# The causal mask of the first key block: from a TensorE product to selections and products on the exponentials

## The chip, the cores and the metric

The kernel runs on one core of a Trainium2 chip. The core has five engines, each of which works through its own queue in order: TensorE (PE; its weight loads are shown as PEld), VectorE (DVE), ScalarE (ACT), GpSimd (POOL) and SyncE (SP, which here only issues transfers). Matrix products are written to PSUM, eight banks of 128 x 512 fp32; all else lies in SBUF. GpSimd does not work on PSUM in this kernel.

The metric is the device time of one execution in microseconds. The kernel before takes 3545.71 us, the median of three runs (3545.69, 3545.71, 3548.17). One more execution was profiled.

## The reference

The input is 32 sequences of 256 tokens with 256 features. First comes a state-space block (a projection, a short convolution, a layer norm, a clipped recurrence over the 256 tokens with 16 states of 512 channels, a gate, a projection back). On its result work two transformer layers with local attention over windows of 128 and a gated feed-forward network. The attention is what the change touches:

```python
def local_attention(q, k, v):                    # 8 heads of 64; WINDOW = 128, so w = 2 windows
    bq = q.reshape(b, h, w, WINDOW, d) * QK_SCALE
    bk, bv = (look_around(bk), look_around(bv))  # the window before, and the own one
    sim = jnp.einsum('bhwid,bhwjd->bhwij', bq, bk)
    mask = (i < j) | (i > j + WINDOW) | (j == -1)
    sim = jnp.where(mask, -jnp.finfo(sim.dtype).max, sim)
    attn = jax.nn.softmax(sim, axis=-1)
    out = jnp.einsum('bhwij,bhwjd->bhwid', attn, bv)
```

With 256 tokens there are two key blocks. The keys of block 0 are seen by the queries of window 0 where the query is not earlier than the key, and by those of window 1 where the query is at most 128 later. So the 128 x 256 scores of key block 0 (keys by queries) keep an upper triangle of the left half and a lower triangle of the right half. Key block 1 is seen by window 1 alone, with one triangle.

## The kernel before

The 32 sequences go in four groups of eight (`NG`, `GB`). For one group `group_scan` (from L379) runs the state-space block: 256 steps, one after the other, each one VectorE instruction over 128 x 512 (`step`, L718) on a row that ScalarE scales (L708) and TensorE reads out (L730). In chunks of 32 steps it prepares the convolution: GpSimd starts an accumulator (`conv_in`, L480), VectorE adds three taps (`conv_taps`, L491). Then the group's eight sequences pass through two layers, so there are 4 x 2 x 8 = 64 passes of one sequence through one layer. The state-space block of group g + 1 runs beside the passes of group g. The last group's 16 passes have nothing beside them.

A pass is spread over eight stages (`ST = 8`), by `attend`, `feed` and `fetch` (L1485 to L1532), and neighbouring passes overlap: while one pass makes scores, the next sequence is projected, the output of the one before is finished, and older ones are in the feed-forward network. What matters here, by stage of pass n:

- Stages 0 to 6, for the next sequence: `project` makes q, k and v of both windows on TensorE (`ps_qkv`, L991); `rotated` (L1000) squares them on ScalarE (L1004), applies the rotary tables on VectorE (L1007, L1012, L1017) and GpSimd (L1015, and the inverse norm `rn` in L1021); `unit` (L1027, VectorE) scales. The second window's rotations are written in stage 4.
- Stage 2: `scores` of the first two head pairs of key block 0 and of all four pairs of key block 1. Stage 3: `scores` of the last two head pairs of key block 0. Scores go into two PSUM banks (one for each head of a pair), and `exponentials` (L1239, ScalarE) turns each bank into an SBUF tile `pT` of 128 x 512. There are six `pT` buffers, as many as one pass uses.
- Stage 3: `mask` of key block 1 by GpSimd's `affine_select` (L1250).
- Stage 7: `sums` (the softmax denominators, L1264) and `values` (L1282), both TensorE on `pT`.
- In the next pass: the denominators go through DRAM and come back inverted and spread (stages 0 to 3), `divide` (stage 5) multiplies the attention output `oT` by them on VectorE (L1322), `finish` (stage 6) projects it (`ps_wo`, L1047).
- Also feed-forward work: gelu products on VectorE (`ag`, L1420), the last addition `fo` of the second layer on VectorE (L1440) and, with the input, on GpSimd (L1448).

The mask of key block 0 is made in two ways. In groups 0 to 2 `open_banks` (L1200) first multiplies a bf16 unit matrix by a bf16 mask of 0 and -32768 into the bank, 128 x 512 for each of the four banks of a pass, and `products` adds the scores on top. Since half of each triangle's square is masked anyway, `products` splits the 128 keys in two halves of 64 and leaves the fully masked quarter out: four matmuls of 64 x 64 weights and 192 queries for a head pair. In the last group (`self.apart`) there is no mask product, a head pair takes two matmuls of 64 x 128 weights and 256 queries, and VectorE multiplies the exponentials by a mask of 0 and 1 (L1255), twice in each of stages 3 and 4.

The program's text gives an order, and a planner makes each engine's queue from it by the dependences and by durations that it estimates: an instruction whose inputs it expects early can be issued ahead of earlier text. `tc.keep_in_program_order` pins an instruction behind everything written before it for its engine. The masks, `divide` and `unit` are pinned so; the rotations and convolution steps are not.

## Time and profile before

| what | value |
|---|---|
| median of three runs | 3545.71 us |
| the profiled execution, its own time | 3553.66 us |
| its span in the trace | 3551.9 us |
| granted TensorE clock, mean | 0.986 |
| busy: TensorE / VectorE / ScalarE / GpSimd | 97% / 73% / 57% / 46% |
| mask products L1200: 192, mean duration | 380 ns |
| score products L1227 of 64 x 64 weights and 192 queries: 1536 records | 335 ns |
| score products L1227 of 64 x 128 weights and 256 queries: 256 records | 402 ns |
| selections L1250, 128 x 512: 128, mean | 853 ns |
| mask products of VectorE L1255, 128 x 512: 64, mean | 817 ns |

The recurrence of the first group runs alone up to about 480 us. From then to about 2790 us passes and recurrence run side by side, and from there to the end the last group's passes run alone.

How to read it: a matmul's duration contains the time to fill and drain the array, and neighbours overlap, so the cost of a row of matmuls is read from its first start to the start of what follows. fp32 matmuls appear as two records each. Waits name the instruction that came last; "idle before" of an engine that is not the bound costs nothing. In order-of-time views the columns are start and duration in us, engine, line, operation, output and inputs, shape, count, and in brackets the idle time before and what ended it.

### The profile page before, as it was taken

What the parts mean: (1) busy time and instruction counts of PE and PEld (TensorE: products, weight loads), DVE (VectorE), ACT (ScalarE), POOL (GpSimd) and SP (SyncE); (2) the same over time, 40 slices, a digit from 0 to 9 for tenths busy, and PEclk for the clock granted to TensorE, in tenths of its full rate; (3) what the DMA queues carried; (4) which work ended last, traced back from release to release, by engine and by line L of the source; (5) the groups of instructions that cost most, each with busy time, mean ns of one, the idle gap of its engine ahead of it and who ended that gap; (6) DMA issues with size and microseconds to landing.
All of it is one profiled execution on the core that took longest, in us unless ns stands there. A gap on an engine that the chain in (4) does not pass through costs nothing.

```text
span 3551.9 us, 57690 instructions
## 1 busy us (share of the span) xinstructions
PE 3441.7 (97%) x20220; PEld 2263.7 (64%) x20220; DVE 2605.5 (73%) x5049; ACT 2037.4 (57%) x3663; POOL 1620.7 (46%) x1587
## 2 busy tenths in 40 slices
PE   7999989999999999999999999999999999999999
PEld 5445335666666666666666666666666777777777
DVE  4888898877878777877787778787777545555563
ACT  3666656656666656666566656666666444444442
POOL 4433455544545445544454556454443333333441
PEclk8999999999999999999999999999999999999999
DMA  6788765534454555544454445544444212011111
GB/s 183 211 219 217 200 174 153 135 113 134 125 143 138 150 144 150 139 121 126 123 144 131 139 147 146 145 115 129 124 138 118 63 37 62 13 31 35 37 28 38
DMA packets 487199, 436.72 MB, mean 123 GB/s; under 512 B 247155, under 2 KB 326516, under 8 KB 486772
## 3 DMA queue, kind: packets, MB, share of 16 engines
q1 hardware_dynamic: 402450, 420.94, 42.0%
q10 hardware_dynamic: 84450, 12.01, 2.1%
q8 instruction: 162, 2.65, 0.3%
q14 instruction: 137, 1.12, 0.1%
HBM read 384.06 MB, written 47.19 MB: 121 GB/s over the span
## 4 chain that ended last, share of the span: by engine, by line
PE 64%; DVE 16%; DMA 7%; ACT 5%; POOL 4%; issue 3%; SPq 1%; ACTq 0%; DVEq 0%; POOLq 0%
PE ps_qkv L991 13%; PE pa L1402 13%; PE po_f L1429 6%; DVE h L718 6%; DMA xrep<-xnd 5%; PE y L730 5%; PE ps_wo L1047 5%; PE ov L1282 4%; PE ps_in L401 3%; PE ps_out L810 3%; PE sc L1227 3%; PE tr_qk L1036 2%; PE rs L1264 2%; ACT xrep L708 2%; DVE acc L491 2%
## 5 line engine op out<-in xcount | busy, mean ns | idle before, releaser
L718 DVE CUSTOM_DVE_ANT_0 h<-h,xrep,lim 128x512 f32<-128x512 f32 x1024 | 931.9, 910 | 215.1 <-ACT xrep L708 166.5
L708 ACT ACTIVATE xrep<-xrep,beta 128x512 f32<-128x512 f32 x960 | 672.5, 720 | 315.7 <-DMA xrep<-xnd 202.4
L991 PE MATMUL ps_qkv<-qkv,res 128*128 128x512 f32 x1536 | 715.2, 601 | 17.2 <-DVE ag L1420 7.2
L1402 PE MATMUL pa<-hT,w 128*128 128x256 f32 (+1 forms) x2816 | 674.5, 382 | 5.4 <-DVE zT L801 5.1
L1402 PEld LDWEIGHTS pa<-hT,w 128*128 128x128 f32 (+1 forms) x2816 | 517.6, 189 | 145.1 <-issue 38.0
L1015 POOL TENSOR_TENSOR rot<-rot,swp 128x512 f32<-128x512 f32 x256 | 349.0, 1363 | 543.7 <-DVE swp L1012 513.0
L991 PEld LDWEIGHTS ps_qkv<-qkv,res 128*128 128x128 f32 x1536 | 282.2, 191 | 299.8 <-issue 242.2
L1021 POOL TENSOR_TENSOR rn<-ss,neg_half 128x8 f32<-128x8 f32 x256 | 461.0, 1801 | 0.0
L1420 DVE SCALAR_TENSOR_TENSOR ag<-pa,b_sb,ag 128x256 f32<-128x256 f32 x320 | 151.9, 475 | 280.0 <-ACT ag L1413 279.7
L730 PE MATMUL y<-h,ly 128*32 128x512 f32 x2048 | 335.8, 606 | 9.8 <-DVE h L718 9.2
L1429 PE MATMUL po_f<-ag,w 128*128 128x256 f32 x1280 | 305.7, 386 | 1.4 <-DVE fo L1440 0.6
L1354 POOL TENSOR_TENSOR rstd<-ve,neg_half 128x2 f32<-128x2 f32 x64 | 46.1, 720 | 555.9 <-DVE ve L1352 555.9
L1429 PEld LDWEIGHTS po_f<-ag,w 128*128 128x128 f32 x1280 | 235.3, 190 | 64.8 <-DVE xc L511 11.7
L1413 ACT ACTIVATE ag<-pa,b_sb 128x256 f32<-128x256 f32 x320 | 149.9, 469 | 217.8 <-PE pa L1402 215.7
L1004 ACT ACTIVATE sq<-ps_qkv,tiny 128x512 f32<-128x512 f32 x256 | 172.4, 685 | 172.2 <-PE ps_qkv L991 143.8
L1047 PE MATMUL ps_wo<-oT,wo 128*128 128x256 f32 x1024 | 236.2, 385 | 14.2 <-DVE oT L1322 11.2
L1047 PEld LDWEIGHTS ps_wo<-oT,wo 128*128 128x128 f32 x1024 | 196.6, 193 | 45.5 <-issue 9.9
L491 DVE SCALAR_TENSOR_TENSOR acc<-xr,wc_sb,acc 128x256 f32<-128x256 f32 x384 | 188.6, 523 | 46.4 <-POOL acc L480 45.9
L1012 DVE TENSOR_TENSOR swp<-ps_qkv,rs_sb 128x256 f32<-128x256 f32 x512 | 191.8, 416 | 29.8 <-POOL rot L1015 29.6
L1007 DVE TENSOR_TENSOR rot<-ps_qkv,rc_sb 128x512 f32<-128x512 f32 x256 | 173.8, 679 | 45.8 <-ACT sq L1004 45.6
L1239 ACT ACTIVATE pT<-sc 128x512 f32<-128x512 f32 x384 | 202.1, 603 | 7.3 <-PE sc L1227 5.5
L1027 DVE SCALAR_TENSOR_TENSOR rot<-rn,rot 128x512 f32<-128x512 f32 x256 | 196.1, 804 | 5.0 <-POOL rn L1021 4.7
(161 smaller groups left out, 5306.9 us busy)
## 6 DMA issues: line engine op xcount, KB each, us to landing
xrep<-xnd SPq DMA_DIRECT2D x960, 256.0 KB
rb<-inv SPq DMA_DIRECT2D x128, 256.0 KB
xnd<-xn SPq DMA_DIRECT2D x64, 256.0 KB
qkv<-in_wqkv_dram SPq DMA_DIRECT2D x24, 512.0 KB
ahead<-xs_a SPq DMA_DIRECT2D x48, 256.0 KB
xp<-ahead SPq DMA_DIRECT2D x48, 256.0 KB
xd<-xnd SPq DMA_DIRECT2D x192, 64.0 KB
w<-in_w_dram SPq DMA_DIRECT2D x80, 128.0 KB
```

Of the source, the lines that this page charges most:

```text
L491: nc.vector.scalar_tensor_tensor(acc, xr[:, :, k : k + CH], wc_sb[:, ch, k : k + 1], acc, ALU.mult, ALU.add,)
L708: scaled = nc.scalar.activation(bx, ck[c].pop(("bx", t), bx), AF.Copy, scale=ck[c]["beta"][:, t : t + 1])
L718: nc.vector._custom_dve(TENSOR_ADD_SAT, out=h_new, in0=state["h"], in1=bx, s0=ck[c]["lim"][:, 0, t : t + 1], s1=ck[c]["lim"][:, 1, t : t + 1],
L730: nc.tensor.matmul(ck[c]["y", hb][32 * q : 32 * q + 32, :], ly[hb % 2][:, 32 * t : 32 * t + 32], ck[c].pop(("h", hb * TB + t)), start=(i = ...
L991: nc.tensor.matmul(ps, res[b][:, k, t0 : t0 + W], wt["qkv", a][:, k], start=(k == 0), stop=(k == KM - 1),)
L1015: nc.gpsimd.tensor_add(rot, rot, swp)
L1021: nc.gpsimd.tensor_tensor(rn, ss, neg_half, ALU.pow)
L1027: nc.vector.scalar_tensor_tensor(rot, bc(rn, 2, DH), 1e12, rot, ALU.min, ALU.mult)
L1047: nc.tensor.matmul(po[:, d], wt["wo", 0][:, c, d * P : (d + 1) * P], oT[:, c, :], start=(c == 0), stop=(c == NC_ - 1),)
L1239: nc.scalar.activation(p, banks[r], AF.Exp)
L1402: nc.tensor.matmul(dst[x], wt["w1", m][:, k, x], self.h[:, k], start=(k == 0), stop=(k == KM - 1),)
L1429: nc.tensor.matmul(self.po[:, d], wt["w2", 0][:, m, d * P : (d + 1) * P], self.ag[m], start=(m == 0), stop=(m == len(MCH) - 1),)
```

## The change

No group makes the mask product any more. `products` takes two matmuls of 64 x 128 weights and 256 queries for a head pair in every group. The mask of key block 0 is put on the exponentials: in groups 0 to 2 the first two head pairs (written in stage 3) by VectorE's product with the mask of 0 and 1, the last two (stage 4) by GpSimd's selection, two `affine_select` for each of two tiles, each over one half of the queries (128 x 2 x 128). In the last group both stay on VectorE. The bf16 unit matrix and the mask of -32768 go, and the mask of 0 and 1 is made directly.

```diff
-    mask_t = const.tile([P, 2 * W], BF, tag="mask_t", name="mask_t")
-    ident_b = const.tile([P, P], BF, tag="ident_b", name="ident_b")
-    nc.vector.tensor_copy(ident_b, ident)
-    nc.gpsimd.memset(mask_t, 0.0)
...
     mask_1 = const.tile([P, 2 * W], BF, tag="mask_1", name="mask_1")
-    nc.gpsimd.tensor_scalar(mask_1, mask_t, -1.0, None, ALU.is_ge)
+    nc.gpsimd.memset(mask_1, 1.0)
+    for i, sign in enumerate((1, -1)):
+        half_1 = mask_1[:, i * W : (i + 1) * W]
+        nc.gpsimd.affine_select(
+            out=half_1, in_=half_1, compare_op=ALU.is_ge, fill=0.0,
+            base=0, pattern=[[sign, W]], channel_multiplier=-sign,
+        )
...
-                self.apart = g == NG - 1
+                self.l, self.last = l, g == NG - 1
...
             def open_banks(self, kw, n):
                 nq = S - kw * W
-                banks = []
-                for r in range(2):
-                    sc = ps_w.tile([P, n, nq], FP, tag="w", name="sc")
-                    if kw == 0 and not self.apart:
-                        nc.tensor.matmul(
-                            sc, ident_b, bc(mask_t[:, 0:nq], 1, n), start=True, stop=False
-                        )
-                    banks.append(sc)
-                return banks
+                return [ps_w.tile([P, n, nq], FP, tag="w", name="sc") for _ in range(2)]
...
-                        for m in range(nm):
-
-                            k0 = m * mk
-                            q0, q1 = (k0, k0 + W + mk) if masked else (0, nq)
-                            nc.tensor.matmul(
-                                banks[r][k0 : k0 + mk, i, q0:q1],
-                                kT[rows, i0 + i, kw * W + k0 : kw * W + k0 + mk],
-                                qT[rows, i0 + i, kw * W + q0 : kw * W + q1],
-                                start=not masked,
-                                stop=not masked or i == n - 1,
-                            )
+                        nc.tensor.matmul(
+                            banks[r][:, i, :],
+                            kT[rows, i0 + i, kw * W : (kw + 1) * W],
+                            qT[rows, i0 + i, kw * W :],
+                            start=True,
+                            stop=True,
+                        )
...
-                    if kw:
-                        masked = nc.gpsimd.affine_select(
-                            out=p, in_=p, compare_op=ALU.is_ge, fill=0.0, base=0,
-                            pattern=[[0, n], [1, W]], channel_multiplier=-1,
+                    if kw == 0 and (i0 == 0 or self.last):
+                        tc.keep_in_program_order(
+                            nc.vector.tensor_mul(p, p, bc(mask_1[:, 0:nq], 1, n))
                         )
-                    else:
-                        masked = nc.vector.tensor_mul(p, p, bc(mask_1[:, 0:nq], 1, n))
-                    tc.keep_in_program_order(masked)
+                        continue
+                    for j in range(nq // W):
+                        sign, part = 1 - 2 * j, p[:, :, j * W : (j + 1) * W]
+                        tc.keep_in_program_order(
+                            nc.gpsimd.affine_select(
+                                out=part, in_=part, compare_op=ALU.is_ge, fill=0.0,
+                                base=0, pattern=[[0, n], [sign, W]],
+                                channel_multiplier=-sign,
+                            )
+                        )
...
             stage(n, 3, at.mask, 1, 0)
-            if at.apart:
-                for i, what in ((3, (0, 0)), (4, (0, 2))):
-                    stage(n, i, at.mask, *what)
+            for i, what in ((3, (0, 0)), (4, (0, 2))):
+                stage(n, i, at.mask, *what)
```

## The prediction

> **What bounds the kernel now.** I read the page first: one line of it says who is full.
>
> ```profile
> PE 3441.7 (97%) x20220; PEld 2263.7 (64%) x20220; DVE 2605.5 (73%) x5049; ACT 2037.4 (57%) x3663; POOL 1620.7 (46%) x1587
> ```
>
> A share over the whole span mixes stages, so the next view is the table of stretches (columns: us, busy of PE, PEld, DVE, ACT and POOL, granted TensorE clock, DMA share, GB/s).
>
> ```profile
> 780.00:800.00 20.00, 18.24 (x131) 13.27 (x132) 16.53 (x26) 7.60 (x14) 7.30 (x7) 0.84 0.56 143
> 980.00:1000.00 20.00, 17.19 (x66) 10.15 (x65) 12.76 (x21) 10.32 (x18) 6.92 (x5) 0.91 0.46 115
> 1800.00:2000.00 200.00, 198.06 (x1240) 131.52 (x1240) 159.61 (x316) 124.96 (x229) 105.80 (x99) 1.00 0.48 134
> ```
>
> From 1000 to 2850 us TensorE idles about 1%, VectorE 20%, GpSimd nearly half. TensorE is the bound there, and what leaves it is worth its length, as long as nothing that it waits for gets later. How near is that? Third view, the waits of TensorE:
>
> ```profile
> PE ps_wo L1047 <- DVE oT L1322: 11.2, 4, 6.1
> ```
>
> The total is small, but a wait list shows no near misses. So the fourth view is the order of time, VectorE and then TensorE, around one output projection `ps_wo` (I number the 64 passes of a sequence through a layer from 0; this is pass 29's):
>
> ```profile
> 2055.19 1.21 DVE L1322 TENSOR_TENSOR oT<-oT,rb 128x1024 f32<-128x1024 f32 x1
> 2056.33 0.68 DVE L1007 TENSOR_TENSOR rot<-ps_qkv,rc_sb 128x512 f32<-128x512 f32 x1
> ...
> 2060.38 0.80 DVE L718 CUSTOM_DVE_ANT_0 h<-h,xrep,lim 128x512 f32<-128x512 f32 x1
> ```
>
> ```profile
> 2054.74 1.99 PE L1402 MATMUL pa<-hT,w 128*128 128x256 f32 x8
> 2056.57 3.67 PE L1047 MATMUL ps_wo<-oT,wo 128*128 128x256 f32 x16
> ```
>
> The division `oT` ends at 2056.40 and `ps_wo` starts at 2056.57: no slack. Measured so for all passes, the distance is 0.05 to 0.27 us at 1, 4, 6, 8, 11, 13, 15, 17, 27, 29, 31 and 33, 1.3 to 1.5 at the other odd ones from 19 to 37, and 1.7 to 9.7 at nearly all even ones. Odd passes carry the recurrence's convolution on VectorE, and there VectorE is right behind TensorE.
>
> **The change, part by part.** *TensorE.* The trace has both forms: groups 0 to 2 open the first key block with mask products, the last group does not. In order of time:
>
> ```profile
> 2033.38 0.59 PE L1200 MATMUL sc<-mask_t,ident_b 128*128 128x512 bf16 x2
> 2033.91 1.97 PE L1227 MATMUL sc<-qT,kT 64*64 64x192 f32 x32
> 2035.81 2.42 PE L1429 MATMUL po_f<-ag,w 128*128 128x256 f32 x10
> ...
> 2038.94 0.59 PE L1200 MATMUL sc<-mask_t,ident_b 128*128 128x512 bf16 x2
> 2039.47 0.88 PE L1227 MATMUL sc<-qT,kT 64*64 64x192 f32 x16
> 2040.28 1.98 PE L991 MATMUL ps_qkv<-qkv,res 128*128 128x512 f32 x4
> ...
> 3131.91 2.02 PE L1227 MATMUL sc<-qT,kT 64*128 64x256 f32 x24
> 3133.86 2.43 PE L1429 MATMUL po_f<-ag,w 128*128 128x256 f32 x10
> ...
> 3137.09 1.13 PE L1227 MATMUL sc<-qT,kT 64*128 64x256 f32 x8
> 3138.15 1.98 PE L991 MATMUL ps_qkv<-qkv,res 128*128 128x512 f32 x4
> ```
>
> From the first scores' start to the next work's, stage 2 falls from 2.43 to 1.95 us and stage 3 from 1.34 to 1.06: 0.75 a pass by the medians over all (0.76 here), times 48 passes, **-36.0 us**. Nothing covers it: this is the bound. In the first ten passes (500 to 1000 us, TensorE busy 469 of 500) part of their 7.5 us may be lost. I count it whole.
>
> *Added work.* VectorE gets two products a pass, and GpSimd four selections over half the width (duration in ns: least, median, most):
>
> ```profile
> L1255 DVE TENSOR_TENSOR pT<-pT,mask x64: 679/683/1764, 2904.0 to 3486.6; 128x512 f32<-128x512 f32 x64
> ...
> L1250 POOL TENSOR_SCALAR_AFFINE_SELECT pT<-pT x128: 628/812/1212, 520.9 to 3480.6; 128x512 f32<-128x512 f32 x128
> ```
>
> That is 2 x 0.683 = 1.37 us on VectorE (66 us in all) and 4 x 0.43, half a selection's mean of 0.853, = 1.7 us on GpSimd (82 us in all). As load alone both fit the idle shares, and the masked tiles are wanted only in stage 7 (in one pass scores at 1538.9, sums at 1562.1 us). What counts is what they push. The products are issued just ahead of `unit` (L1027), then come the convolution taps, the gelu products and the division. In odd passes that run is nearly without gaps, so the division moves with it. Setup loses three small instructions, under 2 us beside the first loads: nothing.
>
> *What moves.* I compared the issue order of the engines as the two kernels are built. TensorE's order between the score products and `ps_wo` stays. VectorE's does not. At passes 6, 13, 15, 17, 27, 29, 31 and 33, and at 2, the two rotations of the next sequence's second half (L1007, L1012, L1017 twice) now come ahead of the division. By the rows above they last 2060.38 - 2056.33 = 4.05 us. Against that, two taps (0.48 each) and one pair of L474 (0.67) go behind it. The division is later by 4.05 + 1.37 - 0.96 - 0.67 = 3.8 us, TensorE comes 0.28 earlier, the slack is 0.17: a wait of 3.9 us. That is the lower end. Seven of these (all but 2 and 6) also have the final addition `fo` (L1448) in GpSimd's queue; the four selections are placed behind it and ahead of two convolution starts (L480) that VectorE's taps wait for, up to 1.7 more: 5.6. The trace even has one case with the rotations ahead, number 4, as the chain of waits and then TensorE's order show:
>
> ```profile
> 776.48 0.60 DVE rot L1007
> ...
> 780.48 1.14 DVE oT L1322
> ```
>
> ```profile
> 781.76 1.62 PE L1047 MATMUL ps_wo<-oT,wo 128*128 128x256 f32 x3 [6.05 <-DVE oT L1322]
> ```
>
> So 3.9 to 6.05 each; I take 4.5, nearer the counted end because number 4 also had a late tap. 8 x 4.5 = 36, and 1.8 at pass 2, whose slack is 2.27: **+37.8 us**. At number 4 the built order now puts the rotations behind the division, 3.7 us of its 6.05: **-3.7**, and its clock loss goes. Passes 1, 8 and 11 have no slack and get 0.5, 1.2 and 0.8 from the products: **+2.5**. Behind each new wait, short waits on VectorE that the trace has now lose their cause (0.72 us for `zT` at 2061.84, the like at six more places): 8 x 0.72, **-5.8**.
>
> *The clock.* The stretch from 780 to 800 us holds the 6.05 us wait and a granted clock of 0.84: 3.2 us lost. 5.48 us at 579 gave 0.86 over 25 us (3.5). Waits of 2.54 us gave 0.91 over 20 us (1.8, in the table above) and 0.83 over 20 (3.4). Two of 2.1 and 2.0 us gave 1.00. A wait of 4.5 lies past the shorter ones that cost 1.8 to 3.4; I take their mean, 2.6: 8 x 2.6, **+21**, bounds 0 and 8 x 3.5 = 28. With number 4's 3.2 back, **-3.2**.
>
> The Trainium skill, "TensorE: Matmul & The Clock Gate", section "What's actually happening", states that the clock falls to half only after at least one idle window of about 3.4 us, and that the window runs freely. By that a 4.5 us gap covers a whole window in about a third of the cases, and half rate for 3.4 us costs 1.7, so an estimate from that page is 8 x 0.32 x 1.7 = 4.4 us instead of 21, and the sum below would be -4. The clock after the two waits of 2.54 us disagrees with the page, so the trace's rows decide.
>
> *Sharing between VectorE and GpSimd.* `h` (L718) lasts 0.80 us alone and 1.11 beside a selection, in the trace's singles. Four half selections may so cost VectorE 0.5 to 0.8 us a pass. Odd passes 19 to 25, 35 and 37 have 1.3 to 1.5 of slack for that; in the eight it lies within the 4.5.
>
> The Trainium skill, "SBUF — State Buffer", section "Who interferes with whom", says that a VectorE instruction with two SBUF inputs contends with a GpSimd one that reads SBUF. The rise of `h` agrees; read as full blocking (its "Terms"), all 1.7 us would go to VectorE in each pass, and an estimate for the eight passes is 8 more us.
>
> **Sum.** -36.0 + 37.8 - 3.7 + 2.5 - 5.8 + 21 - 3.2 = +12.6 us. The profiled execution took 3553.66 us (span 3551.9, 1.8 around it), 8 us above the median of 3545.71; carried to the median: **3558 us**, +0.35%. From no change a measurement of this kernel can tell about 0.2%, 7 us.
>
> **Rivals.** *TensorE's saving comes through (faster).* The place is the division: if VectorE reaches it early enough, because its run starts as much earlier as TensorE gets ahead or the reordered rotations fill time it would idle, the waits do not arise. Price: -36 + 2.5 + about 5 for odd spots, 3517 us. The point from which it decides: the other terms of the sum come to -44.4, so it is faster where the eight passes cost under 5.5 us each, clock included (I have 4.5 + 2.6). For it: TensorE 1% idle, VectorE 20%. Against: 0.17 us of slack, and number 4.
>
> *It cancels.* Waits of 3.9 us (31) with half the clock losses (10) against the -44.4: -3 us, 3543, within 0.2%.
>
> *GpSimd becomes a second bound (slower, more).* Each pass delays rotation or convolution by the 1.7 us of its selections, and VectorE with it. At half of the 24 odd passes that is 20 us more, 3578. For it: VectorE already waits 45.9 us for `acc` from L480. Against: GpSimd idles 513 us ahead of L1015, and 2.7 us ahead of L480 in the odd passes at 1542 and 2043 us, where selections fit.
>
> *The change does less than it says*: the masked work is in the built order, so this is no case.
>
> **How the numbers follow.** Chances: the sum's case 0.42, through 0.28, cancel 0.15, second bound 0.15. The sum's case alone runs from 3550 (4.2 us each and 1.9 of clock) to 3574 (6.05 and 3.0). For 8 in 10 the range reaches into "through" down to 3519, and up to 3582. Faster by over 0.2%: 0.30; within: 0.16; slower: 0.54.
>
> **What would show it.** Right: no L1200 row, scores from start to start at 1.95 and 1.06 us everywhere; TensorE's wait for `oT` up from 11 to about 45 us with new waits of 4 to 6 us at those eight passes; clock below 1.00 behind them, in stretches after 1020 us that now show 1.00; VectorE's rotation ahead of `oT`. Wrong: that wait stays near 11 us, or waits for `acc` or `rn` from GpSimd grow. The weakest step is that the built order meets the same arrival times as before.

## The result: 1.5% slower

The changed kernel takes 3598.15 us (median of 4 runs, 3595.80 to 3601.68), the kernel before 3546.3 in the same comparison (4 runs). The ratio is 1.015, 95% interval 1.0135 to 1.0164: 52 us slower. The forecast had 3558 us and a range up to 3582: the sign is right, the size is not. The profiled execution took 3601.68 us, with a span of 3599.9.

The page of the changed kernel (busy time, share and instructions of each engine):

```profile
PE 3435.1 (95%) x19260; PEld 2278.6 (63%) x19260; DVE 2665.7 (74%) x5144; ACT 2037.4 (57%) x3663; POOL 1712.7 (48%) x1778
```

TensorE has 960 instructions less, and yet its busy time hardly moved, which an unchanged clock would not give (the mean granted clock is 0.979, against 0.986 before). VectorE has 60 us more and GpSimd 92. The stretches (us, busy of PE, PEld, DVE, ACT, POOL, granted clock, DMA share, GB/s) show where TensorE lost its full clock. From 1800 to 2000 us it was busy 198 us at 1.00 before. Now the clock dips, and the two short rows show one such dip behind the output projection of pass 29:

```profile
1800.00:2000.00 200.00, 188.81 (x1077) 127.01 (x1079) 159.01 (x313) 121.96 (x224) 106.61 (x107) 0.98 0.48 131
2094.00:2098.00 4.00, 1.01 (x3) 0.87 (x4) 3.74 (x6) 0.00 (x0) 4.00 (x4) 0.50 0.13 51
2098.00:2102.00 4.00, 4.00 (x14) 3.31 (x13) 3.95 (x11) 0.94 (x2) 3.25 (x2) 0.66 0.30 95
```

The waits of the changed kernel (us in total, times, longest). The first was 11.2 us in 4 times before; the second, VectorE for GpSimd's convolution start, was 45.9 in 96:

```profile
DVE acc L483 <- POOL acc L472: 75.0, 94, 3.2
PE ps_wo L1039 <- DVE oT L1302: 61.3, 16, 6.5
```

The added rows, in ns (least, median, most): the selections of L1231 are the new half ones and the older whole ones together.

```profile
L1231 POOL TENSOR_SCALAR_AFFINE_SELECT pT<-pT x320: 402/702/3200, 517.8 to 3528.7; 128x256 f32<-128x256 f32 x96, 128x512 f32<-128x512 f32 x64
L1225 DVE TENSOR_TENSOR pT<-pT,mask x160: 674/684/1762, 517.0 to 3534.7; 128x512 f32<-128x512 f32 x160
```

Pass 29 again, in order of time, the changed kernel. TensorE first (scores, and then the projection):

```profile
2068.28 2.02 PE L1201 MATMUL sc<-qT,kT 64*128 64x256 f32 x24
2070.23 2.43 PE L1409 MATMUL po_f<-ag,w 128*128 128x256 f32 x10
...
2073.45 1.13 PE L1201 MATMUL sc<-qT,kT 64*128 64x256 f32 x8
2074.52 1.99 PE L983 MATMUL ps_qkv<-qkv,res 128*128 128x512 f32 x4
...
2088.99 1.99 PE L1382 MATMUL pa<-hT,w 128*128 128x256 f32 x8
2096.99 5.31 PE L1039 MATMUL ps_wo<-oT,wo 128*128 128x256 f32 x15 [6.01 <-DVE oT L1302]
```

VectorE, at the same time:

```profile
2085.12 0.76 DVE L466 TENSOR_TENSOR xr<-xp,cond_sb 128x256 f32<-128x256 f32 x2
2089.03 0.48 DVE L483 SCALAR_TENSOR_TENSOR acc<-xr,wc_sb,acc 128x256 f32<-128x256 f32 x1 [3.15 <-POOL acc L472]
...
2091.56 0.68 DVE L999 TENSOR_TENSOR rot<-ps_qkv,rc_sb 128x512 f32<-128x512 f32 x1
...
2095.62 1.22 DVE L1302 TENSOR_TENSOR oT<-oT,rb 128x1024 f32<-128x1024 f32 x1
```

And GpSimd, first in the kernel before and then in the changed one:

```profile
2049.76 1.34 POOL L480 TENSOR_SCALAR acc<-xr,wc_sb,bconv_sb 128x256 f32<-128x256 f32 x2
2051.07 1.27 POOL L1448 TENSOR_TENSOR fo<-fo,xs 128x512 f32<-128x512 f32 x1
```

```profile
2084.63 2.38 POOL L1428 TENSOR_TENSOR fo<-fo,xs 128x512 f32<-128x512 f32 x1
2086.96 1.49 POOL L1231 TENSOR_SCALAR_AFFINE_SELECT pT<-pT 128x256 f32<-128x256 f32 x4
2088.44 0.56 POOL L472 TENSOR_SCALAR acc<-xr,wc_sb,bconv_sb 128x256 f32<-128x256 f32 x1
```

TensorE is free at 2090.98 and waits 6.01 us for a division that begins at 2095.62. Two things stand ahead of it. The rotations take 4.06 us (2091.56 to 2095.62), and before them VectorE idles 3.15 us, since GpSimd's convolution start is now queued behind `fo` and the four selections; before, it stood ahead of `fo`. The waits at passes 15, 17, 27, 29, 31 and 33 are 6.01 us, at 13 6.52.

### The profile page after: what moved, and what is told of

Same layout as the page of the kernel before. It is cut to its first block, busy times and chain, and to the rows that moved or that the text cites. A ratio compares the mean times of both kernels' runs of the same rounds, so it can differ in the third digit from the quotient of the medians.

```text
span 3599.9 us, 56082 instructions
## 1 busy us (share of the span) xinstructions
PE 3435.1 (95%) x19260; PEld 2278.6 (63%) x19260; DVE 2665.7 (74%) x5144; ACT 2037.4 (57%) x3663; POOL 1712.7 (48%) x1778
## 3 DMA queue, kind: packets, MB, share of 16 engines
q8 instruction: 155, 2.54, 0.3%
## 4 chain that ended last, share of the span: by engine, by line
PE 65%; DVE 14%; ACT 6%; DMA 6%; POOL 5%; issue 3%; SPq 0%; ACTq 0%; POOLq 0%; DVEq 0%
PE ps_qkv L983 13%; PE pa L1382 13%; PE ps_wo L1039 6%; PE po_f L1409 6%; DVE h L710 5%; PE y L722 5%; PE ov L1262 4%; DMA xrep<-xnd 4%; PE sc L1201 3%; PE ps_out L802 3%; PE ps_in L393 3%; PE tr_qk L1028 3%; PE rs L1244 2%; DVE acc L483 2%; ACT xrep L700 2%
## 5 line engine op out<-in xcount | busy, mean ns | idle before, releaser
L1039 PE MATMUL ps_wo<-oT,wo 128*128 128x256 f32 x1024 | 258.5, 410 | 65.3 <-DVE oT L1302 61.3
L1039 PEld LDWEIGHTS ps_wo<-oT,wo 128*128 128x128 f32 x1024 | 211.0, 208 | 106.5 <-issue 59.0
L1231 POOL TENSOR_SCALAR_AFFINE_SELECT pT<-pT 128x512 f32<-128x512 f32 x320 | 236.5, 770 | 28.8 <-ACT pT L1213 26.8
L1201 PE MATMUL sc<-qT,kT 64*128 64x128 f32 (+1 forms) x2048 | 202.9, 337 | 2.6 <-DVE swp L1004 1.8
```

What stands on the lines that cost most here:

```text
L1039: nc.tensor.matmul(po[:, d], wt["wo", 0][:, c, d * P : (d + 1) * P], oT[:, c, :], start=(c == 0), stop=(c == NC_ - 1),)
L1201: nc.tensor.matmul(banks[r][:, i, :], kT[rows, i0 + i, kw * W : (kw + 1) * W], qT[rows, i0 + i, kw * W :], start=True, stop=True,)
L1231: nc.gpsimd.affine_select(out=part, in_=part, compare_op=ALU.is_ge, fill=0.0, base=0, pattern=[[0, n], [sign, W]], channel_multiplier=-sign,)
```

## The experiments

The theories: **order** (the rotations ahead of the division make the loss), **load** (the added work lengthens VectorE's run or GpSimd's queue in passes that have no room), and, under both, **saving** (what TensorE gains by the left-out mask products is worth 36 us). Each run has its own runs of the kernel before on the same chip; "against before" below is the difference of the two medians.

**1. The order undone.** A list `held` collects the eight VectorE instructions of the second-window rotations; each gets an ordering edge (no wait) to the division.

```diff
+            if w == 1:
+                held.extend(turned)     # rot, swp, swp, ss of L999 to L1009
...
-                tc.keep_in_program_order(
+                divided = tc.keep_in_program_order(
                     nc.vector.tensor_mul(self.o[b], self.o[b], self.rb)
                 )
+                for ins in held[-8:]:
+                    queue_behind(ins, divided)
+                held.clear()
```

> The changed kernel, with one thing undone: the eight VectorE instructions of the next sequence's second-window rotations are queued behind the division in every pass, as the kernel before had them at passes 13, 15, 17, 27, 29, 31 and 33. Products and selections stay. Order theory (the rotations ahead of the division make the 6 us waits): each of the seven passes gets back the 4.05 us of the rotations and most of its clock dip, pass 6 and pass 2 about 4 together, so 3598 - 7 x 4.05 - 4 - some 5 for the clock = about 3561 us (3555 to 3570), and TensorE's wait for oT falls from 61 us to 20 or less. Load theory (GpSimd's selections ahead of the convolution starts and the products hold the taps, and the rotations only fill that idle time): VectorE idles ahead of the taps instead, the waits for oT stay at 4 to 6 us at those passes, 3585 to 3598 us. By neither is it below the 3546 us of the kernel before, because the steady pairs of passes 19 to 26 and 35 to 38 also lost 1.7 us each and hold no reordered rotation.

Measured: 3570.36 us against 3544.93, ratio 1.0064 (1.0043 to 1.0086). Of the 53 us (3598.15 less 3544.93), 28 are gone and 25 are left. TensorE's wait for `oT` falls to 13.1 us in the list of waits. The list puts 10.5 us more of the projection's waits down to ScalarE, though there too the division ended only 0.1 to 0.15 us before the projection; with these it is 23.6, against 65.2 in the changed kernel counted alike. At pass 29 the projection now waits 1.92 us instead of 6.01: 4.09 less, where the rotations take 4.06. So order is half of the loss, and the other half stands without it.

**2. The order alone.** The kernel before, with the edge the other way round at seven passes.

```diff
+                if divisions[0] in (13, 15, 17, 27, 29, 31, 33):
+                    for ins in held[-8:]:
+                        queue_behind(divided, ins)
```

> The kernel before with its mask products on TensorE, nothing added, and one thing forced: at passes 13, 15, 17, 27, 29, 31 and 33 the division is queued behind the rotations of the next sequence's second window. Order theory: 0.17 us of slack and 4.05 us of rotations give a wait for oT of 3.9 us at each of the seven, 27 us, and a clock loss of 0 to 3 us behind each that is partly hidden: 3546 + 27 to 3546 + 48, about 3580 us. Rival (the order matters only because the added products and selections leave no room): VectorE catches up within the pass and the waits are under 1 us, 3546 to 3553 us.

Measured: 3572.09 us against 3544.93, ratio 1.0076 (1.0048 to 1.0103): +27.2 us, or 3.9 per pass. Its waits, and TensorE in order of time at pass 29:

```profile
PE ps_wo L1060 <- DVE oT L1335: 38.7, 11, 6.0
```

```profile
2064.93 5.46 PE L1060 MATMUL ps_wo<-oT,wo 128*128 128x256 f32 x12 [3.88 <-DVE oT L1335]
```

4.05 us of rotations less 0.17 of slack are 3.88 us, as measured, and the forecast's lower end was 3.9. From one projection's start to the next the seven passes are longer by 3.96 to 4.17 us. What is missing is the clock. Its dip is there:

```profile
2060.00:2064.00 4.00, 1.05 (x5) 0.57 (x4) 3.74 (x9) 3.25 (x6) 3.00 (x3) 0.99 0.56 142
2064.00:2068.00 4.00, 3.07 (x7) 2.52 (x8) 4.00 (x6) 0.00 (x0) 4.00 (x3) 0.50 0.41 146
2068.00:2072.00 4.00, 4.00 (x17) 3.28 (x16) 3.19 (x9) 0.97 (x3) 1.20 (x1) 0.66 0.74 198
```

But the seven passes that follow are in sum 1.5 us shorter than before (longer by -0.34, -2.13, -0.13, -0.10, +0.54, +0.16, +0.49), where 7 x (2.6 - 0.72) = 13 us more were forecast. Two things nearly cancel here. The half clock lasts 6.83 us at passes 29, 31 and 33, 3.41 us at 13, 17 and 27, and at 15, behind a wait of 3.89 us, the clock stays at 1.00. The pass behind number 15 takes 47.06 us, those behind the short dips 48.75, those behind the long ones 49.93 to 49.97, and none of them has a wait of TensorE over 0.2 us ahead of its own projection. So a dip costs its pass 1.7 or 2.9 us, some 14 in all, not far from the forecast's 7 x 2.6 = 18. Against it, the waits that fall away are worth more than the 0.72 us each that the forecast gave them: the pass without a dip is 2.13 us shorter than before. In pass 30 the trace of before has waits of 0.72, 0.68 and 0.34 us (for `zT`, `ag` and `xd`), and here there are none: TensorE, late by the long wait, comes to these places when the data is there.

**3. The saving alone.** The masks of the first key block are left out in groups 0 to 2 (so the result is not the reference's), order held.

```diff
-            for i, what in ((3, (0, 0)), (4, (0, 2))):
-                stage(n, i, at.mask, *what)
+            if at.last:
+                for i, what in ((3, (0, 0)), (4, (0, 2))):
+                    stage(n, i, at.mask, *what)
```

> The changed kernel without any mask of the first key block in groups 0 to 2 (neither product nor selection: what the reference masks there is left in), and with the rotations held behind the division. This is TensorE's saving alone. If the saving arrives whole, as the sum of the forecast had it: 3546 - 36 = 3510 us, and 2 to 4 less for the order at passes 4 and 11. Rival (VectorE follows right behind TensorE in the passes with the recurrence, so what TensorE saves is waited for again): only the passes without a recurrence and the early ones gain, 3535 to 3546 us, with new short waits of TensorE for zT, ag, xd and oT.

Measured: 3534.85 us against 3544.93, ratio 0.9964 (0.9951 to 0.9977): -10.1 us, not -36. Two things came off. The saving itself is smaller than 0.75 us a pass. In passes 41 to 46, where nothing waits, the changed kernel's passes are shorter by 0.46 to 0.66. Pass 43 in order of time, before and then after, shows it:

```profile
2730.39 1.99 PE L401 MATMUL ps_in<-xg,w_in_sb 128*128 128x256 f32 x8
2732.22 0.59 PE L1200 MATMUL sc<-mask_t,ident_b 128*128 128x512 bf16 x2
...
2734.64 2.43 PE L1429 MATMUL po_f<-ag,w 128*128 128x256 f32 x10
```

```profile
2780.83 1.99 PE L393 MATMUL ps_in<-xg,w_in_sb 128*128 128x256 f32 x8
2782.75 2.02 PE L1201 MATMUL sc<-qT,kT 64*128 64x256 f32 x24
2784.70 2.42 PE L1409 MATMUL po_f<-ag,w 128*128 128x256 f32 x10
```

From the start of the work ahead to the start of the work behind, 4.25 us become 3.87: 0.38, where start of scores to next work gave 2.43 - 1.95 = 0.48. The scores start 1.92 us behind the start of `ps_in`, the mask product started 1.83 behind it. At the other scores it is the same (1.77 to 1.59, 0.18 instead of 0.28). So 0.56 to 0.66 a pass, 48 x 0.6 = 29 us (27 to 32).

And of these 29 most is waited for again. Pass 24 (in both, from the projection of pass 23 to its own), TensorE's waits over 0.2 us, in the kernel before and then without masks:

```profile
1756.24 3.62 PE L1047 MATMUL ps_wo<-oT,wo 128*128 128x256 f32 x16
1775.70 1.99 PE L991 MATMUL ps_qkv<-qkv,res 128*128 128x512 f32 x4 [0.53 <-DVE ag L1420]
1785.93 1.99 PE L991 MATMUL ps_qkv<-qkv,res 128*128 128x512 f32 x4 [0.34 <-DVE xd L781]
```

```profile
1747.20 3.62 PE L1052 MATMUL ps_wo<-oT,wo 128*128 128x256 f32 x16
1767.08 1.98 PE L983 MATMUL ps_qkv<-qkv,res 128*128 128x512 f32 x4 [0.90 <-DVE ag L1416]
1775.49 1.13 PE L1214 MATMUL sc<-qT,kT 64*128 64x256 f32 x8 [0.26 <-DVE swp L1015]
1777.31 1.98 PE L983 MATMUL ps_qkv<-qkv,res 128*128 128x512 f32 x4 [0.68 <-DVE xd L773]
```

0.87 us of waits became 1.84. The odd passes keep their 0.55 us, the even ones from 20 to 36 gain nothing (-0.2 to +0.6). The even passes have up to 9.7 us of slack at the projection, but none in the middle, at `ag` and `xd`.

**4. The added work alone.** The mask products stay on TensorE; products and selections are added on top; order held.

```diff
-            if at.apart:
-                for i, what in ((3, (0, 0)), (4, (0, 2))):
-                    stage(n, i, at.mask, *what)
+            for i, what in ((3, (0, 0)), (4, (0, 2))):
+                stage(n, i, at.mask, *what)
```

> The kernel before with its mask products on TensorE kept, and the two VectorE products and four GpSimd selections a pass added on top (they mask again what is masked already), rotations held behind the division. This is the added work alone, without the saving and without the reordering. If it lies beside other work, as shares of 73 and 46 per cent suggest: 3546 to 3550 us. If VectorE's run from the scores to the division is a bound in the odd passes: 1.4 us of products and up to 1.7 us of a delayed convolution start at some 20 odd passes, 3546 + 28 to 3546 + 60, about 3580 us. If VectorE's run sets the time, this kernel and the one with the saving and held rotations come out within 10 us of each other; if TensorE sets it, they are 36 us apart.

Measured: 3577.45 us against 3544.93, ratio 1.0091 (1.0067 to 1.0114): +32.5 us, with a wide spread (3567.6 to 3584.7). It lies 7 us above the run with the saving and held rotations, not 36, nor the 29 of experiment 3. So the run of VectorE and GpSimd, and not TensorE, sets most of the time here. Pass 24 of the run with held rotations (experiment 1) shows how it is paid, in small coin:

```profile
1761.85 3.69 PE L1052 MATMUL ps_wo<-oT,wo 128*128 128x256 f32 x16 [0.61 <-DVE oT L1315]
1767.14 1.99 PE L1398 MATMUL pa<-hT,w 128*128 128x256 f32 x8 [0.73 <-DVE zT L793]
1783.13 1.99 PE L983 MATMUL ps_qkv<-qkv,res 128*128 128x512 f32 x4 [1.27 <-DVE ag L1416]
1791.54 1.13 PE L1214 MATMUL sc<-qT,kT 64*128 64x256 f32 x8 [0.25 <-DVE swp L1015]
1793.36 1.98 PE L983 MATMUL ps_qkv<-qkv,res 128*128 128x512 f32 x4 [0.68 <-DVE xd L773]
```

From these traces I took the time from one projection's start to the next and set it against the kernel before (us, single executions; the first row is the least certain). What lies ahead of pass 0 is in no row, and differs from before by +0.4 us (changed) to -14.1 (run 4, whose trace is its fastest execution), so a column need not add up to the difference of the medians.

| passes | changed | 2: order alone | 1: order held | 3: no mask | 4: work alone |
|---|---|---|---|---|---|
| 0 to 12 | +6.9 | -1.1 | -3.0 | -6.8 | -0.7 |
| 12 to 18 | +15.6 | +9.7 | +8.1 | -0.6 | +7.1 |
| 18 to 26 | +7.1 | +0.4 | +7.2 | -1.3 | +8.0 |
| 26 to 34 | +17.9 | +17.2 | +6.7 | -2.1 | +9.1 |
| 34 to 40 | +3.7 | 0.0 | +3.6 | +0.4 | +3.8 |
| 40 to 48 | -3.5 | 0.0 | -3.5 | -3.6 | +0.2 |

The order acts where the reordered passes are (13 to 17, 27 to 33). The added work costs some 1 us a pass, on average, from 12 to 40, also where no order changed. The saving arrives in 40 to 48, where no recurrence runs.

**5. Each half of the added work.** Order held, and one half left out.

```diff
                     n, nq = p.shape[1:]
+                    if kw == 0 and i0 == 0 and not self.last:    # no products
+                        continue
```

> The changed kernel with the rotations held behind the division, and without the two VectorE products a pass (heads 0 to 3 stay unmasked in the first key block in groups 0 to 2); the four GpSimd selections stay. The same kernel with both kinds of work took 3570 us, with neither 3535. Product theory (1.37 us more on VectorE in a run without slack, some 20 to 25 passes): this one comes to about 3542 us. Selection theory (GpSimd's queue holds back the convolution starts): it stays at about 3562 to 3570 us, with VectorE's wait for acc still near 72 us.

```diff
                     n, nq = p.shape[1:]
+                    if kw == 0 and i0 and not self.last:         # no selections
+                        continue
```

> The changed kernel with the rotations held behind the division, and without the four GpSimd selections a pass (heads 4 to 7 stay unmasked in the first key block in groups 0 to 2); the two VectorE products stay. Product theory: about 3562 to 3570 us. Selection theory: about 3542 us, with VectorE's wait for acc back from 72 to about 46 us. If each takes half, this and the run without products lie both near 3553 us.

Measured: 3550.82 us without products (1.0018, 1.0008 to 1.0028), 3548.40 without selections (1.0008, 0.9999 to 1.0018), both against 3543.36. Neither engine is the one culprit. Each taken against its own runs of before, the selections alone stand 17.5 us above the run without masks (+7.5 and -10.1), the products alone 15.1 (+5.0 and -10.1), and both together 35.5 (+25.4 and -10.1). The 3 us over their sum are within the noise of these differences.

**6. The place of the added work.** The changed kernel pins each mask instruction behind what its engine was given before it in the program. Here this is lifted for the first key block (not for the second), for the products as shown and for the selections of L1231 likewise.

```diff
-                        tc.keep_in_program_order(
-                            nc.vector.tensor_mul(p, p, bc(mask_1[:, 0:nq], 1, n))
-                        )
+                        nc.vector.tensor_mul(p, p, bc(mask_1[:, 0:nq], 1, n))
```

> The changed kernel, whole, with the products and the selections of the first key block no longer pinned behind what was traced before them on their engines, so that the planner places them: the built order then has the products ahead of other scan work in an idle spot, the convolution starts ahead of fo in GpSimd's queue, and the division ahead of the rotations at passes 13 to 33 again (they stay ahead of it at 1, 4, 6 and 11). If the place of the added work was the loss: waits for oT at the seven passes fall from 6 us to under 1, and the time to 3535 to 3555 us. If the load itself is what VectorE and GpSimd cannot bear in the odd passes: 3565 to 3580 us, as with held rotations alone (3570).

Measured: 3583.25 us against 3543.36, ratio 1.0106 (1.009 to 1.0123). It is 40 us slower than before and above both cases, though the planner has the division ahead of the rotations again at the passes from 13 on. By the trace, passes 12 to 40 are at +11 us instead of +44, but passes 0 to 12 at +13.3, and 48 to 63, which the change does not touch, at +9.4: 0.72 us in most passes of the last group. Its waits, the second of which was 4.7 us in 4 times before:

```profile
DVE acc L483 <- POOL acc L472: 34.2, 85, 2.8
DVE rot L1019 <- POOL rn L1013: 23.1, 23, 2.8
```

The last group's products, unpinned, go ahead of `res`, and `unit` behind them now waits for `rn`. So with the order mended at these passes and the convolution starts on time, the kernel was still slow, at others.

**7. The division earlier.** With unpinned masks, the division is traced a stage earlier, and so comes ahead of the second half's taps, the gelu product and the rotations.

```diff
-            stage(n + 1, 5, at.divide, b)
+            stage(n + 1, 4, at.divide, b)
```

> The same as the run with unpinned masks, and the division traced one stage earlier, ahead of the taps, the gelu product and the rotations. If TensorE's waits at the output projection were what was left, the division's 1.2 us then lie well ahead of it at all passes: 3530 to 3545 us, wait for oT under 3 us. If what was pushed behind it (the gelu product and the taps, then the rotations) is waited for instead: waits for ag and for the first rotations of the next turn grow by what oT lost, 3550 to 3575 us.

Measured: 3558.41 us, ratio 1.0037 (1.0026 to 1.0049). In the trace no projection waits for `oT` any more. With the last group's products pinned again:

```diff
+                        masked = nc.vector.tensor_mul(p, p, bc(mask_1[:, 0:nq], 1, n))
+                        if self.last:
+                            tc.keep_in_program_order(masked)
```

> The changed kernel, whole, with the division traced one stage earlier, and the masks of the first key block unpinned in groups 0 to 2 only; in the last group the products stay pinned, as in the changed kernel. The run with all masks unpinned and the early division took 3558 us and lost 0.72 us at each of the 13 passes from 47 to 59 and 61 of the last group's stretch, and some 3 in the passes 40 to 47, against the changed kernel. If these come back: 3558 - 12.5 = about 3546 us (3540 to 3552), level with the kernel before. If the loss of the last group came from the early division and not from the unpinned products: 3555 to 3560 us.

Measured: 3544.44 us against 3543.15, ratio 1.0005 (0.9995 to 1.0015): level with the kernel before, and some 50 us better than the change as it was made, with the same work.

**8. The same place without the change, and without masks.** The edit of 7 in the kernel before, and in the kernel of experiment 3 (there instead of the held rotations).

```diff
-            stage(n + 1, 5, at.divide, b)
+            stage(n + 1, 4, at.divide, b)
```

> The kernel before, its mask products on TensorE, with one thing changed: the division is traced one stage earlier. If the division's place is worth something by itself (it is right behind TensorE's need in 12 passes, with 0.05 to 0.27 us to spare, and what waits behind it is not missed), 3535 to 3543 us; if the gelu product, the taps and the rotations that it pushes back are missed, 3546 to 3556 us. Against the run with the change and the early division it shows what the change of the mask is worth where the division is out of the way: nothing if they are level, at most the 10 us that the run without any mask gained if VectorE and GpSimd had room for the added work.

> The kernel without any mask of the first key block in groups 0 to 2 (what the reference masks there is left in), with the early division: TensorE's saving alone, now with VectorE's last step ahead of the output projection out of the way. If the saving was lost at the output projection: 3510 to 3518 us. If it is lost at other places, where TensorE takes from VectorE in the even passes (zT, ag, xd and bank releases): 3528 to 3536 us, as with the division in its old place (3535).

Measured: 3549.28 us for the first (1.0015, 1.0006 to 1.0024), and 3518.74 for the second (0.993, 0.9913 to 0.9947), against 3543.15. I had expected the second at 3528 to 3536, and missed: where the division comes early, leaving the mask out is worth 30.5 us, all of the 29 that TensorE has to give. Of TensorE's waits over 0.2 us pass 24 keeps one:

```profile
1736.10 3.62 PE L1039 MATMUL ps_wo<-oT,wo 128*128 128x256 f32 x16
1764.77 1.98 PE L983 MATMUL ps_qkv<-qkv,res 128*128 128x512 f32 x4 [0.68 <-DVE xd L773]
```

The early division alone makes the kernel before slower by 6 us (even passes +0.8 to +2.0 from 20 to 36), and the one without masks faster by some 15. Why the two together do what neither does alone isn't settled: the built orders of the two also differ in the place of a few taps, which I did not hold fixed. Against the early division alone, the whole change with unpinned masks is worth 5 us (3549.28 to 3544.44): 30.5 saved on TensorE, 26 paid for the masks.

**9. Both repairs of the order at once.** Rotations held as in 1 and masks unpinned but for the last group.

```diff
+                for ins in held[-8:]:
+                    queue_behind(ins, divided)
...
+                        if self.last:
+                            tc.keep_in_program_order(masked)
```

> The changed kernel, whole, with the rotations held behind the division in every pass and the masks of the first key block unpinned in groups 0 to 2. Held alone gave 3570 us, unpinned alone 3583, of which 9.4 us were lost in the last group and some 16 in passes 1 to 12, where the rotations still came first. If the two act on different losses: 3583 - 12 - 16 = about 3555 us. If the unpinned masks lose as much as they gain, 3565 to 3575 us.

Measured: 3560.21 us, ratio 1.0046 (1.003 to 1.0062): better than held alone by 8 us (each against its own runs of before), but 16 behind the early division.

**10. Which engine, which pins.** All with the early division: the masks pinned as the change had them; pinned in passes 0 to 12 and from 40 on; and so pinned with all heads on one engine.

```diff
+            at.pinned = not 13 <= n < 40
...
-                    if kw == 0 and (i0 == 0 or self.last):
+                    if kw == 0:                     # all on VectorE
+                    if kw == 0 and self.last:       # or: all on GpSimd
```

> The changed kernel, whole and with its masks pinned as they are, with the division traced one stage earlier and nothing else. With masks unpinned in groups 0 to 2 it took 3544 us, without masks 3519. If the place of the masks in the queues is what costs (GpSimd's selections ahead of the convolution starts, products ahead of unit): the passes 13 to 40 lose some 15 us against the unpinned ones, passes 1 to 12 gain up to 8, together 3548 to 3556 us. If only the amount of work counts: level with the unpinned one, 3540 to 3548 us.

> The changed kernel, whole, with the early division, and the masks of the first key block pinned in passes 0 to 12 and from 40 on, unpinned in between. In passes 0 to 12 the unpinned masks stood at +5 us against the kernel before, the pinned ones (with held rotations) at -3; in passes 45 and 46 unpinned ones lost 0.7 each. If these are separate: 3544 - 8 - 1.4 = about 3535 us (3531 to 3540), under the 3543 of the kernel before. If the early passes were better because of the held rotations and not because of the pins: 3542 to 3546 us.

> As the run with the early division and mixed pins, but all heads of the first key block are masked by VectorE's products (four a pass, 2.73 us) and none by GpSimd. If VectorE's load is what costs: 8 to 15 us more than with the halves, 3543 to 3552 us. If GpSimd's selections, or their meeting with VectorE, cost more than a product does: level with the halves or below, 3528 to 3537 us.

> As the run with the early division and mixed pins, but in groups 0 to 2 all heads of the first key block are masked by GpSimd's selections (eight a pass, 3.4 us) and none by VectorE. If VectorE's load is what costs: below the halves, 3522 to 3532 us. If GpSimd's queue is what costs (conv starts and the sums of the rotations stand behind the selections): 8 to 20 us above the halves, 3543 to 3555 us, with VectorE's waits for acc and rn from GpSimd grown.

Measured, against 3545.26: pinned 3562.64 (1.0046, 1.003 to 1.0061), mixed 3549.21 (1.0011, 1.0000 to 1.0021), all on VectorE 3566.45 (1.0057, 1.0042 to 1.0073), all on GpSimd 3576.68 (1.0087, 1.0068 to 1.0106). The pins cost some 16 us (17.4 against the 1.3 of the unpinned run), and the pinned run lies above both cases. Keeping them in passes 0 to 12 brought nothing (I had expected 3535): these passes stand at +8.3 in the trace, at +5.1 unpinned, and at -9.5 with the early division and no masks. So it is the added work together with the early division that is paid there, and not the lifted pins. On either engine alone the masks cost 17 to 27 us more than in halves, and both runs lie above their expected ranges. With all on GpSimd, VectorE's wait for `acc` is 49.1 us, hardly more than the 46 of before, so the convolution start, to which I had put that case's price, isn't its cause. What is, I did not follow further.

**11. The best pieces.** Division late with held rotations and pinned masks in passes 0 to 12, early and unpinned from 13, pinned again from 40.

```diff
-            stage(n + 1, 5, at.divide, b)
+            stage(n + 1, 5 if n < 13 else 4, at.divide, b, n < 13)   # n < 13: held
```

> The changed kernel, whole: for the first 13 sequences the division stays in its old stage, with the rotations held behind it and the masks pinned; from then on the division is traced one stage earlier and the masks are unpinned, and pinned again from pass 40. If the stretches are separate: -3 us in passes 0 to 12, about -6 in 12 to 40, -3.5 in 40 to 48, together some 12 us under the kernel before, 3530 to 3538 us. If a gain in the first stretch is waited for again in the second: 3543 to 3550 us, level with the kernel before.

Measured: 3543.15 us against 3545.38, ratio 0.9989 (0.9979 to 0.9999). Passes 0 to 12 came out at -0.4 instead of -3, and 34 to 40 at +0.4. It is faster than the changed kernel by 1.5%, and than the kernel before by 0.1%, within what I had called no change.

## Why the forecast had the sign and missed the size

By medians the account closes: saving -10.1, added work with the order held +35.5 (3534.85 to 3570.36), order +27.8 (3570.36 to 3598.15): +53.2, and 3598.15 - 3544.93 is 53.2. It closes by construction, each step being the difference of two neighbouring runs. What supports the split is that the two costs come out alike on the kernel before: the order alone +27.2, the added work on top of the mask products +32.5. The forecast's sum, cut in the same way, was -36, about +2.5 and +46.1 (37.8 - 3.7 - 5.8 + 21 - 3.2): wrong by 26 and 33 one way and by 18 the other.

The sign owes much to luck. Without the clock and the waits that fall away the forecast's terms are -36.0 + 37.8 - 3.7 + 2.5 = +0.6, no change; "slower" came from +21 - 3.2 - 5.8 = +12 for these two. In the run of the order alone they came to -1.5 us at its seven passes. With that in its place the same sum would have said no change. The waits for the division were forecast rightly as a loss, but what lets them show is that most of the saving did not come (-10.1), and the rest of the loss is the added work, which the forecast had at +2.5.

- **TensorE's -36, counted whole: failed, by 26.** "Nothing covers it: this is the bound" was read from one place. I measured the slack of VectorE at the output projection alone, and took 1.7 to 9.7 us there in the even passes for room. The binding places of an even pass are in its middle (`ag`, `xd`, `zT`, banks freed by `swp`), and they had shown themselves in the trace of before as waits of 0.3 to 1.4 us. They bind only with the division at its place: a stage earlier, the same saving came whole (30.5 us, experiment 8), and why is open. Seven of the 26 are of another kind: I measured from the scores' start, and not from the start of the work ahead of them.
- **The added work, "as load alone both fit the idle shares": failed, by 33.** This is the largest error. I had bounded the products' price at the passes without slack at the projection only. In experiment 4 the odd passes 19 to 25, with their 1.3 to 1.5 us of slack there, lose 0.5 to 1.1 us each, and the even passes 20 to 26, with still more, 1.1 to 1.6. It is not that the engines slow each other down, the *Sharing* of the forecast: by the traces the durations of VectorE's instructions other than those on `pT` add up to 2866.7 us before and 2861.5 in the changed kernel, those of GpSimd to 1549.4 and 1511.1. The price is waiting, and it depends on the place: 35.5 us with the order held, 26 with the division early and the masks unpinned.
- **The rotations: right in place and mechanism.** The waits came at the eight passes named; 3.88 us where the order alone changed, against 3.9 counted. With the selections ahead of the convolution starts they were 6.0 to 6.5, above the 4.5 taken and near number 4's 6.05. Pass 6 waits 4.89 (1.08 of it was there before), pass 4 falls from 6.05 to 1.27, more than the 3.7 forecast, and pass 2 (3.62) waits twice the 1.8.
- **The clock, +21, and the waits that fall away, -5.8: near in the first, failed in the second.** In the changed kernel the granted clock fell to 0.50 for 6.83 us behind all eight waits; in the order-only run for 6.83, 3.41 or no time at all, 2.0 us a pass in the mean against 2.6. The waits that fall away were put at 0.72 each. They were 1.74 at pass 30, and the one pass without a dip was 2.13 shorter. One of the rows that the forecast went by was misread: the clock of 0.83 over 20 us (from 500 us) stands behind waits of 2.13, 1.05 and 2.83 us, not one of 2.54. The Trainium skill ("TensorE: Matmul & The Clock Gate", section "What's actually happening") puts half clock behind at least one idle window of about 3.4 us. The stretches of 3.41 us agree with its window. That the window must be idle does not agree, if idle means without any work: in the order-only run TensorE was busy for 0.07 to 0.34 of the 3.41 us ahead of the six dips, and in the rows at the end for 0.44.
- **The rivals.** "Through" and "it cancels" fell with the -44.4 that both rest on, and not with the waits: all reordered rotations together cost 27.8 us, 3.5 for each of the eight passes with the clock in it, under the 5.5 from which "through" was to win. "GpSimd becomes a second bound" was the one nearest in size (3578). Its sign, VectorE's wait for `acc`, went from 45.9 to 75.0 us, and without the selections 20 us come back. But it was not GpSimd alone, as without the products 18 come back. The signs that I had named for being right came, with waits of 4.9 to 6.5 us instead of 4 to 6 and 61 us in all instead of 45; so did one of those for being wrong, the growing wait for `acc`, and I had not priced the case that both come.

## What to carry to other kernels

A second engine that is 75% busy can still have no room: measure its distance to the bound engine at every place where that takes something from it, in every kind of pass, and take waits of 0.3 us as a hint of a place that can take what the bound engine saves. Where small work is added to two engines, compare the built order around each handover, and try the pins and the stage of the last step first: here the same change of the mask cost 52 us in one place and 1 in another. Price a new wait with what it sets off, the drop of the clock and the later waits that fall away: here these nearly cancelled (+14 and -15 us at seven passes).

## What was not expected of the hardware

Behind a wait of 1.92 us at pass 29 of experiment 1 (held rotations) the clock fell to half. Behind the same 1.92 us at pass 27 it stayed at 1.00, as it did in the trace of before behind waits of 2.1 and 2.0 us. In the traces the half clock comes in stretches of 3.41 us or whole multiples of it, and within one execution their starts lie on one grid of 3.41 us. These are the stretches of that grid around the two waits (us, busy of PE, PEld, DVE, ACT and POOL, granted clock, DMA share, GB/s), pass 27 and then pass 29:

```profile
1962.19:1965.60 3.41, 2.48 (x16) 1.44 (x8) 2.44 (x6) 2.29 (x5) 1.60 (x5) 1.00 0.60 179
1965.60:1969.01 3.41, 2.42 (x11) 2.19 (x12) 3.30 (x6) 0.95 (x2) 1.15 (x1) 1.00 0.08 31
1969.01:1972.43 3.42, 2.69 (x17) 2.19 (x17) 3.27 (x7) 0.00 (x0) 3.42 (x4) 1.00 0.00 0
2067.99:2071.41 3.42, 1.50 (x8) 1.25 (x8) 3.42 (x7) 2.02 (x5) 0.11 (x1) 1.00 0.74 267
2071.41:2074.82 3.41, 3.41 (x10) 2.65 (x9) 3.15 (x7) 0.00 (x0) 3.41 (x3) 0.50 0.13 50
```

The wait at pass 27 is split over two stretches, and TensorE is busy for 2.4 us or more of each. The wait at pass 29 falls into one and leaves 1.50 us of it. From 500 to 3500 us of six traces (before, changed, experiments 1, 2, 4 and 6), of the stretches at full clock the 47 with half clock behind them had TensorE busy for at most 0.44 of their length, and the some 5150 others for at least 0.42. So the length of one wait does not tell whether the clock falls; where it lies on the grid matters as well. The busy share is not the whole rule: in the run without masks (experiment 3) half clock at 1071 us follows a stretch that was busy for 0.69.
